# The third state of a gated graph network turned by DMA instead of TensorE, with layer 1 one step later

## The chip, the cores and the metric

The kernel runs on one core of a Trainium2 chip. The metric is the device time of one launch in microseconds (us); for the kernel before, three runs gave a median of 2498.61 us (2496.37 to 2498.63). All times below are in us unless they are marked ns.

## The reference

There are 64 graphs of 256 nodes with 256 features each, and an int32 adjacency per graph. Two pre-norm layers follow one another:

```
h = relu(layernorm(x))
for i in range(3):                       # layer 0: gated graph network, 3 steps
    m    = h @ weight[i]
    aggr = A^T @ m                       # A = (adj != 0)
    h    = gru_cell(aggr, h)             # r, z = sigmoid(..), n = tanh(..); (1-z) n + z h
x = x + h
h = relu(layernorm(x))                   # layer 1: graph attention, 4 heads of 64
v = h W^T + b
l = leaky_relu(v.a_src + v.a_dst, 0.2);  l = -9e15 where adj != 1
x = x + softmax(l) v
```

## The kernel before

**Tiling.** Two graphs form a pair (`PB = 2`), so there are 32 pairs (`NPAIR`) of 512 nodes. The state `hT_a` lies turned, features on partitions and nodes along the free axis (`[128, 2, 512]`), which is what the gate products need. The input `x`, the sum with `aggr` and layer 1 need it by nodes, 128 nodes on the partitions (`[128, 4, 256]`).

**Order.** The order on every engine is written out by hand. `at(tick, phase, p, fn)` files a piece of work under a tick and one of three phases (STEP, READY, REST); at the end all ticks are emitted in order, within a phase the newest pair first. Every engine runs its own instructions in the order in which they are emitted. A step of the gated network takes six ticks (`SUB = 6`, functions `tick_0` to `tick_5`), then `update` writes the new state in place (lines L557 to L559). A pair starts every 18 ticks (`APART`), at `t0 = 18 p`. Its three steps start at t0, t0+12 and t0+24, so the steps of neighbouring pairs fill each other's gaps, and a period of 18 ticks holds three slots. This document calls them:

- slot A, ticks 0 to 5 of the period: the first step of the newest pair
- slot B, ticks 6 to 11: the third step of the pair before it
- slot C, ticks 12 to 17: the second step of the newest pair

Layer 1 of older pairs, and the layer norm and loads of younger ones, are filed into the same ticks.

**Within a step.** TensorE writes gate sums into PSUM banks, and VectorE fills some banks in between: `pe` (L510: `pd + m5`, after which `tick_4` writes into `pd` again) and `pn0`, `pn1` (`first_n`, L526: `(R + 1) * hn`, on top of which `input_n` accumulates). In `tick_5` TensorE's order is `pn0`, `pd`, `pn1`. VectorE also evicts the turned state into `hNlo` (L799) after ScalarE has written `hNhi` (L798). GpSimd makes `hT - n` for the first graph (L541).

**The state by nodes.** After every step `back(l, i)` turns the state by nodes with TensorE, four 128x128 transposes into a bank for each graph (L808, `turn_back`). After the third step `residual` (L814) adds that bank to `x` on VectorE, at ticks t0+31 and t0+32, in slot C.

**Turning by DMA.** For most pairs the normalized input is turned by `plan_turn` in three pieces: `halve` (L387) splits the float32 words into 16-bit halves on VectorE and writes them to DRAM (L389, on SyncE's queue, SP), `turn` reads them back with a DMA transpose (L393), `join` (L399) puts the halves together on VectorE. This is done for layer 0 (`a`) and layer 1 (`b`), with one buffer each for `words` and `turned`.

**Layer 1.** `plan_norm` (L341, L342 statistics; L353 result), `plan_turn`, `values` (L864), `score_rows` (rows to DRAM and back onto all partitions, L893 and L907), `barred_in` and `leaky` (ScalarE), `maxima` (L949, VectorE, two SBUF inputs), `exps` (ScalarE), `output`: `product` on TensorE (L573) and `divided` (L582, L584 on VectorE, L589 on GpSimd). `bar` (L838) makes the mask of absent edges out of a second load of the adjacency; `to_edge` (L764) makes the one for layer 0. `later` moves the ticks of layer 1.

Of the kernel before, what the change touches and what calls it, by code (L numbers as in the profile page):

```python
# [12 lines left out]
U16 = mybir.dt.uint16  # L13
# [5 lines left out]
P = 128  # L19
# [8 lines left out]
def gated_gnn_then_gat_kernel(  # L28
# [39 lines left out]
    nc = tc.nc  # L68
    B, N, D = x.shape
    L = weight.shape[0]  # L70
# [3 lines left out]
    KD = D // P  # L74
    KN = N // P
    PB = 2
    R = PB * KN
    T = PB * N
# [3 lines left out]
    NPAIR = B // PB  # L82
# [6 lines left out]
    dram = ctx.enter_context(tc.tile_pool(name="rows", bufs=2, space=bass.MemoryType.DRAM))  # L89
# [8 lines left out]
    def bank(name):  # L98
        return ps_m.tile([P, 512], F32, tag="mm", name=name)

    BUFS = {
        "x": 5, "adj": 2, "edge": 2, "noedge": 2, "hT_a": 2, "xn": 2, "val": 2, "row": 2, "zz": 4, "o": 2,
    }
# [219 lines left out]
    SUB = 6  # L323
# [3 lines left out]
    def at(tick, phase, p, fn):  # L327
        plan.setdefault(tick, ([], [], []))[phase].append((-p, fn))

    def plan_norm(src, name, p, ticks, relu=False):  # L330


        v = {}

        def stats(r0):
            def fn():
                if not v:
                    v["st"] = small.tile([P, R, 6], F32, tag="st", name=f"st_{name}")
                    v["mv"] = small.tile([P, R, 2], F32, tag="mv", name=f"mv_{name}")
                for r in (r0, r0 + 1):  # L340
                    nc.vector.bn_stats(v["st"][:, r, :], src()[:, r, :])  # L341
                    nc.vector.bn_aggr(v["mv"][:, r, :], v["st"][:, r, :])  # L342
            return fn

        def deviation():
            rstd = v["rstd"] = small.tile([P, R], F32, tag="rstd", name=f"rstd_{name}")
            nc.vector.tensor_scalar_add(rstd, v["mv"][:, :, 1], EPS)
            nc.gpsimd.tensor_tensor(rstd, rstd, mhalf, ALU.pow)

        def result():  # L350
            xn = v["xn"] = buf("xn", [P, R, D], f"xn_{name}")
            for r in range(R):
                nc.vector.tensor_scalar(  # L353
                    xn[:, r, :], src()[:, r, :], v["mv"][:, r, 0:1], 0.0 if relu else v["rstd"][:, r : r + 1],
                    op0=ALU.subtract, op1=ALU.max if relu else ALU.mult,
                )

        for t, fn in zip(ticks, (stats(0), stats(2), deviation, result)):
            at(t, READY, p, fn)
        return v  # L360

    def plan_relu_T(v, tag, name, p, ticks):
# [12 lines left out]

        for k, t in enumerate(ticks):
            at(t, REST, p, fn(k))
        return w

    def plan_turn(src, tag, name, p, ticks):  # L380


        w = {}

        def halve():
            words = buf("words", [P, R, 2, D], f"words_{name}", U16)
            nc.vector.tensor_copy(words, src().bitcast(U16).rearrange("q r (d w) -> q r w d", w=2))  # L387
            w["rows"] = dram.tile([R, P, 2 * D], U16, tag="words", name=f"words_dram_{name}")
            nc.sync.dma_start(w["rows"].rearrange("r q e -> q r e"), words.rearrange("q r w d -> q r (w d)"))  # L389

        def turn():
            w["turned"] = buf("turned", [P, 2, KD * T], f"turned_{name}", U16)
            nc.sync.dma_start_transpose(  # L393
                w["turned"].rearrange("q w (k n) -> q (w k) n", k=KD), w["rows"].rearrange("r q e -> (r q) e")
            )

        def join():
            w["hT"] = buf(tag, [P, KD, T], f"hT_{name}")
            nc.vector.tensor_copy(  # L399
                flat(w["hT"]).bitcast(U16).rearrange("q (n w) -> q n w", w=2), w["turned"].rearrange("q w n -> q n w")  # L400
            )
# [339 lines left out]
    def plan_pair(p):  # L741
        t0 = APART * p
        v = {}
        last = p == NPAIR - 1
        late = p == NPAIR - 2

        def ready(t, fn):
            at(t0 + t, READY, p, fn)

        def step(t, fn):  # L750
            at(t0 + t, STEP, p, fn)

        def rest(t, fn):
            at(t0 + t, REST, p, fn)


        if p == 0:
            v["x"], v["adj"] = first
        else:
            rest(-16, lambda: v.update(x=load_x(p), adj=load_adj(p, "adj")))  # L760

        def to_edge():
            v["edge"] = buf("edge", [P, R, N], f"edge_{p}", F32R)
# [5 lines left out]
        xn_a = plan_norm(lambda: v["x"], f"a{p}", p, [t0 + t for t in norm_ticks])  # L769
        ready(-1 if p else -2.5, to_edge)  # L770
        if dma_a:
            ready(-9.5, lambda: nc.scalar.activation(flat(xn_a["xn"]), flat(xn_a["xn"]), AF.Relu))
            h = plan_turn(lambda: xn_a["xn"], "hT_a", f"a{p}", p, [t0 - 9, t0 - 8, t0 - 3])
        else:
            h = plan_relu_T(xn_a, "hT_a", f"a{p}", p, [t0 - 4, t0 - 3])

# [12 lines left out]
        def back(l, i):  # L789

            def fn():
                if l < L - 1 and i == 0:
                    v["hN"] = node_halves(f"{p}_{l}")
                turn_back(l, i)
                pt = v["pback", i]
                hi, lo = (flat(y[:, i * KN : (i + 1) * KN, :]) for y in v["hN"])
                if l < L - 1:
                    nc.scalar.copy(hi, pt)  # L798
                    nc.vector.tensor_sub(lo, pt, hi)  # L799
                else:  # L800
                    residual(i)
            return fn

        def turn_back(l, i):
            pt = v["pback", i] = bank(f"pback_{p}_{l}_{i}")
            for s in range(KN):
                for k in range(KD):
                    nc.tensor.transpose(  # L808
                        pt[:, s * D + k * P : s * D + (k + 1) * P], h["hT"][:, k, ts(i * KN + s, P)], ident
                    )  # L810

        def residual(i):
            xi = flat(v["x"][:, i * KN : (i + 1) * KN, :])
            nc.vector.tensor_add(xi, v["pback", i], xi)  # L814

        for l in range(L):
            end = last and l == L - 1
            g = Step(f"{p}_{l}", l, lambda: h["hT"], end)
            t = 2 * SUB * l
            ready(t - 3 if l else t - 1, g.state_sums)  # L820
            ready(t + 2, g.last_state_sum)
            step(t, lambda g=g: g.tick_0(v["hN"], v["edge"]))
            for k, fn in enumerate((g.tick_1, g.tick_2, g.tick_3, g.tick_4, g.tick_5), 1):
                step(t + k, fn)
            if not end:
                ready(t + SUB, lambda g=g: g.update(0))
                ready(t + SUB, lambda g=g: g.update(1))
                for i in range(PB):
                    rest(t + SUB + 1 + i, back(l, i))


        def load_adj_1():
# [8 lines left out]
                nc.sync.dma_start(v["noedge_rows"].rearrange("r q t -> q r t"), v["noedge"])  # L841

        rest(16 if last else 22, load_adj_1)
        ready(28 if last else 35, bar)
        if last:
            plan_tail(t0, p, v, g, lambda i: turn_back(L - 1, i), residual)
            return

        dma_b = p < NPAIR - 3
        later = SUB if dma_b else 0  # L850
        xn_b = plan_norm(lambda: v["x"], f"b{p}", p, [t0 + 32, t0 + 33, t0 + 33, t0 + 34], dma_b)
        if dma_b:
# [48 lines left out]
        rows, drow, logits = {}, {}, {}  # L901
# [74 lines left out]
        for y in range(R * H // 2):  # L976
            r, h0 = divmod(2 * y, H)
# [90 lines left out]
```

## Time and profile before

| what | value |
|---|---|
| median of three runs | 2498.61 us |
| profiled execution, its own time | 2498.09 us |
| its span in the profile | 2496.3 us |
| granted TensorE clock | 0.997 |
| TensorE matmul busy | 2464.2 us, 99% |
| TensorE weight load busy | 2191.9 us, 88% |
| VectorE busy | 1992.2 us, 80% |
| ScalarE busy | 1437.5 us, 58% |
| GpSimd busy | 494.3 us, 20% |
| transposes of L808 | 768, of 273 ns each |
| GpSimd sums of L541 (128x512) | 96, of 1479 ns each |
| GpSimd sums of L589 (128x256) | 124, of 1107 ns each |

The duration of a matmul is that of one instruction; matmuls overlap, and so the distance between the starts of neighbours says what each costs. PE stands for TensorE, DVE for VectorE, ACT for ScalarE, POOL for GpSimd, and SPq for SyncE's sequencer. In steady state a period of three slots lasts 75.5 us.

### The profile page before, as it was taken

To read this page: it belongs to the slowest core of one execution; us is meant where nothing else is said; L and a number is where in the kernel's file an instruction comes from. 1 tells how busy PE (TensorE), PEld (TensorE's weight loads), DVE (VectorE), ACT (ScalarE), POOL (GpSimd) and SP (SyncE) were. 2 spreads that over 40 slices of the span, in tenths; PEclk is the share of its full clock that TensorE was granted. 3 is DMA by queue.
4 is the path that set the end of the run, shared out by engine and by line. 5 is a ranking of instruction groups with operands and counts; after the bars stand their busy time and mean duration, and the time that the engine had idled before them with its cause. 6 is when DMAs were issued, how large, how long until landed. Compare 5 with 4: busy or idle time off the path is not lost.

```text
span 2496.3 us, 37566 instructions
## 1 busy us (share of the span) xinstructions
PE 2464.2 (99%) x13446; PEld 2191.9 (88%) x13446; DVE 1992.2 (80%) x4671; ACT 1437.5 (58%) x3007; POOL 494.3 (20%) x419
## 2 busy tenths in 40 slices
PE   8999999999999999999999999999999999999998
PEld 6888888888988888988888988888888889888887
DVE  5678877888877888777888778888778888778767
ACT  3445556555556555566565566565565555665664
POOL 0011121221221121212121212121212222212212
PEclk9999999999999999999999999999999999999999
DMA  3025656455656456656556565556565556564455
GB/s 95 9 68 119 152 119 153 121 127 134 136 127 155 119 126 143 132 131 147 116 131 148 117 146 138 116 130 147 122 153 127 123 132 140 125 157 118 107 109 110
DMA packets 322090, 313.72 MB, mean 126 GB/s; under 512 B 166560, under 2 KB 282224, under 8 KB 321904
## 3 DMA queue, kind: packets, MB, share of 16 engines
q0 software_dynamic: 33728, 130.03, 27.4%
q1 hardware_dynamic: 286608, 181.29, 27.0%
q8 instruction: 106, 1.74, 0.3%
q14 instruction: 80, 0.66, 0.1%
q10 hardware_dynamic: 1568, 0.01, 0.0%
HBM read 215.62 MB, written 56.60 MB: 109 GB/s over the span
## 4 chain that ended last, share of the span: by engine, by line
PE 83%; DVE 12%; ACT 3%; issue 1%; DMA 1%; POOL 0%; SPq 0%; ACTq 0%; DVEq 0%; POOLq 0%
PE pd L313 18%; PE pn L313 13%; PE pc L313 9%; PE po L573 8%; PE pe L313 7%; PE pa L470 5%; PE qb L448 5%; PE p L313 5%; PE pv L864 5%; PE qa L448 4%; PE pback L808 2%; DVE hT_a L559 2%; DVE any L949 2%; DVE R L558 2%; DVE hNlo L799 1%
## 5 line engine op out<-in xcount | busy, mean ns | idle before, releaser
L313 PE MATMUL pn<-aggr,w_a 128*128 128x256 f32 x1536 | 364.9, 380 | 2.8 <-DVE pn L526 2.8
L313 PE MATMUL pd<-T,w_a 128*128 128x256 f32 x1536 | 366.4, 382 | 0.0
L541 POOL TENSOR_TENSOR R<-hT_a,hn 128x512 f32<-128x512 f32 x96 | 141.9, 1479 | 1124.5 <-ACT hn L537 1042.5
L313 PEld LDWEIGHTS pn<-aggr,w_a 128*128 128x128 f32 x1536 | 286.9, 190 | 44.3 <-DVE pn L526 2.1
L313 PEld LDWEIGHTS pd<-T,w_a 128*128 128x128 f32 x1536 | 288.1, 191 | 37.6
L573 PEld LDWEIGHTS po<-val,zz 128*128 128x128 f32 x2048 | 244.9, 192 | 4.5
L537 ACT ACTIVATE hn<-pn,bi 128x256 f32<-128x256 f32 x384 | 160.4, 470 | 145.6 <-PE pn L313 145.4
L589 POOL TENSOR_TENSOR x<-x,o 128x256 f32<-128x256 f32 x124 | 137.1, 1107 | 538.3 <-DVE o L584 538.3
L558 DVE SCALAR_TENSOR_TENSOR R<-Z,R 128x512 f32<-128x512 f32 x192 | 132.5, 690 | 137.9 <-POOL R L541 126.3
L573 PE MATMUL po<-val,zz 128*128 128x65 f32 x2048 | 242.1, 272 | 0.0
L969 ACT ACTIVATE zz<-zz,val 128x256 f32<-128x256 f32 x496 | 223.7, 505 | 0.0
L949 DVE CUSTOM_DVE_ANT_0 any<-drow,noedge 128x256 f32<-128x256 f32 x496 | 209.1, 422 | 9.3 <-DMA drow<-score_dram 0.5
L455 ACT ACTIVATE R<-pc,brz 128x256 f32<-128x256 f32 x192 | 80.5, 470 | 230.8 <-PE pc L313 230.8
L526 DVE SCALAR_TENSOR_TENSOR pn<-R,hn 128x512 f32<-128x512 f32 x192 | 149.1, 777 | 77.3 <-ACT R L455 54.7
L455 ACT ACTIVATE R<-pe,brz 128x256 f32<-128x256 f32 x192 | 80.4, 470 | 213.5 <-PE pe L313 213.5
L313 PE MATMUL pd<-T,w_h 128*128 128x256 f32 x768 | 184.4, 383 | 3.1 <-DVE pe L510 0.4
L313 PE MATMUL pc<-aggr,w_a 128*128 128x256 f32 x768 | 182.5, 381 | 0.0
L313 PE MATMUL p<-T,w_a 128*128 128x256 f32 x768 | 181.9, 379 | 0.6 <-DVE w_a L247 0.6
L313 PE MATMUL pe<-aggr,w_a 128*128 128x256 f32 x768 | 181.4, 379 | 0.0
L313 PE MATMUL pc<-hT_a,w_h 128*128 128x256 f32 x768 | 181.4, 379 | 0.0
L799 DVE TENSOR_TENSOR hNlo<-pback,hNhi 128x512 fp32r<-128x512 f32 x128 | 88.2, 689 | 110.9 <-ACT hNhi L798 110.9
L313 PEld LDWEIGHTS pd<-T,w_h 128*128 128x128 f32 x768 | 143.5, 190 | 32.8 <-DVE pe L510 14.5
(183 smaller groups left out, 5323.0 us busy)
## 6 DMA issues: line engine op xcount, KB each, us to landing
zz<-score_dram POOLq DMA_DIRECT2D x62, 1024.0 KB, 11.0
zz<-topT_dram POOLq DMA_DIRECT2D x62, 1024.0 KB, 7.9
adj<-in_adj_dram SPq DMA_DIRECT2D x64, 512.0 KB
drow<-score_dram SPq DMA_DIRECT2D x62, 512.0 KB
x<-in_x_dram SPq DMA_DIRECT2D x32, 512.0 KB
out_dram<-x SPq DMA_DIRECT2D x31, 512.0 KB
words_dram_a<-words_a SPq DMA_DIRECT2D x30, 512.0 KB
words_dram_b<-words_b SPq DMA_DIRECT2D x29, 512.0 KB
```

The source lines that it names most:

```text
L313: nc.tensor.matmul(pt[:, ts(c, N)], w[:, k, j * D + c * P : j * D + (c + 1) * P], src[:, k, :], start=start and c == 0 and k == 0, stop=(c ...
L448: nc.tensor.matmul(pt, w_n[:, j, :], src, start=start, stop=True, skip_group_check=True)
L455: nc.scalar.activation(of(dst, i)[:, c, :], src[:, c, :], AF.Tanh, bias=brz[:, g0 + c : g0 + c + 1], scale=0.5)
L470: nc.tensor.matmul(pt[:, ts(i, N)], hN[half][:, i * KN + s, ts(e, P)], edge[:, i * KN + s, :], start=(s == 0 and half == 0), stop=(s == KN ...
L526: nc.vector.scalar_tensor_tensor(by_c(self.bank(f"pn{i}")), of(self.R, i), 1.0, of(self.hn, i), op0=ALU.add, op1=ALU.mult)
L537: nc.scalar.activation(n__[:, c, :], p_n[:, c, :], AF.Tanh, bias=bi[:, 2 * KD + c : 2 * KD + c + 1])
L541: nc.gpsimd.tensor_sub(of(self.R, i), of(self.hT(), i), n__)
L558: nc.vector.scalar_tensor_tensor(d_, of(self.Z, i), 1.0, d_, op0=ALU.add, op1=ALU.mult)
L573: nc.tensor.matmul(po[:, ts(h_, VC)], zz[:, j, h_, ts(s, P)], v["val"][:, i * KN + j, ts(h_, VC)], start=(j == 0), stop=(j == KN - 1),)
L589: add(v["x"][:, r, :], v["x"][:, r, :], o)
L949: nc.vector.tensor_tensor_reduce(any_, drow[r // KN][:, h, :], v["noedge"][:, r, :], 1.0, -3.0e38, ALU.add, ALU.max, accum_out=v["top"][:, ...
L969: nc.scalar.activation(zz[:, h, :], zz[:, h, :], AF.Prelu, alpha=ALPHA, bias=v["val"][:, r, S0 + H + h : S0 + H + h + 1],)
```

## The change

For the first 27 pairs (`home`, p < 27) the third state is no longer turned by TensorE. VectorE splits it into halves, the halves go to DRAM, a DMA transpose brings them back by nodes, and VectorE joins them in a buffer of the tag `xn`. GpSimd, instead of VectorE, adds the result to `x`, in one instruction of 128x1024. Layer 1 of these pairs starts six ticks later than before, so each of its pieces moves on by one slot. `bar` comes seven ticks earlier, the pieces of `plan_turn` for layer 0 one tick later. The adjacency has one buffer instead of two, its first load is filed at t0-5 instead of t0-16, and `x` has six buffers instead of five.

```diff
-        "x": 5, "adj": 2, ...
+        "x": 6, "adj": 1, ...
...
-            rest(-16, lambda: v.update(x=load_x(p), adj=load_adj(p, "adj")))
+            rest(-16, lambda: v.update(x=load_x(p)))
+            rest(-5, lambda: v.update(adj=load_adj(p, "adj")))
...
-            h = plan_turn(lambda: xn_a["xn"], "hT_a", f"a{p}", p, [t0 - 9, t0 - 8, t0 - 3])
+            h = plan_turn(
+                lambda: xn_a["xn"], lambda: buf("hT_a", [P, KD, T], f"hT_a{p}"), f"a{p}", p, [t0 - 8, t0 - 7, t0 - 2]
+            )
...
+        home = p < NPAIR - 5
+        if home:
+            h_3 = plan_turn(
+                lambda: h["hT"], lambda: buf("xn", [P, R, D], f"h_{p}"), f"h{p}", p, [t0 + 33, t0 + 34, t0 + 37]
+            )
+            ready(37, lambda: nc.gpsimd.tensor_add(v["x"], v["x"], h_3["hT"]))
...
                 for i in range(PB):
-                    rest(t + SUB + 1 + i, back(l, i))
+                    if not (home and l == L - 1):
+                        rest(t + SUB + 1 + i, back(l, i))
...
-        ready(28 if last else 35, bar)
+        ready(28, bar)
...
-        later = SUB if dma_b else 0
-        xn_b = plan_norm(lambda: v["x"], f"b{p}", p, [t0 + 32, t0 + 33, t0 + 33, t0 + 34], dma_b)
+        later = 2 * SUB if home else SUB if dma_b else 0
+        t_n = t0 + SUB if home else t0
+        ticks = [t_n + (32.5 if home else 32), t_n + 33, t_n + 33, t_n + 34]
+        xn_b = plan_norm(lambda: v["x"], f"b{p}", p, ticks, dma_b)
         if dma_b:
-            hb = plan_turn(lambda: xn_b["xn"], "hT_b", f"b{p}", p, [t0 + 34.1, t0 + 35, t0 + 41])
+            hb = plan_turn(
+                lambda: xn_b["xn"], lambda: buf("hT_b", [P, KD, T], f"hT_b{p}"), f"b{p}", p,
+                [t_n + 34.1, t_n + 35, t_n + 41],
+            )
...
-        rest(37 if dma_b else 36, linked)
+        rest((36, 37, 43)[later // SUB], linked)
```

`plan_turn` itself takes its shapes from its source now (two blocks of 512 for the state, four of 256 for the normalized input); the instructions for `a` and `b` keep their shapes.

More of the change, by code (lines that the diff above doesn't have):

```diff
@@ L101, in gated_gnn_then_gat_kernel @@
     BUFS = {
-        "x": 5, "adj": 2, "edge": 2, "noedge": 2, "hT_a": 2, "xn": 2, "val": 2, "row": 2, "zz": 4, "o": 2,
+        "x": 6, "adj": 1, "edge": 2, "noedge": 2, "hT_a": 2, "xn": 2, "val": 2, "row": 2, "zz": 4, "o": 2,
     }
@@ L378, in plan_relu_T, with plan_turn @@
         return w
-    def plan_turn(src, tag, name, p, ticks):
+    def plan_turn(src, dst, name, p, ticks):
         w = {}
         def halve():
[L386 to L389, printed above, removed]
+            y = src()
+            nb, n = y.shape[1:]
+            words = buf("words", [P, nb, 2, n], f"words_{name}", U16)
+            nc.vector.tensor_copy(words, y.bitcast(U16).rearrange("q b (n w) -> q b w n", w=2))
+            w["rows"] = dram.tile([nb, P, 2 * n], U16, tag="words", name=f"words_dram_{name}")
+            nc.sync.dma_start(w["rows"].rearrange("b q e -> q b e"), words.rearrange("q b w n -> q b (w n)"))
         def turn():
[L392 to L395, printed above, removed]
+            nb, _, n2 = w["rows"].shape
+            w["turned"] = buf("turned", [P, n2 // P, nb * P], f"turned_{name}", U16)
+            nc.sync.dma_start_transpose(w["turned"], w["rows"].rearrange("b q e -> (b q) e"))
         def join():
-            w["hT"] = buf(tag, [P, KD, T], f"hT_{name}")
+            w["hT"] = dst()
             nc.vector.tensor_copy(
-                flat(w["hT"]).bitcast(U16).rearrange("q (n w) -> q n w", w=2), w["turned"].rearrange("q w n -> q n w")
+                flat(w["hT"]).bitcast(U16).rearrange("q (n w) -> q n w", w=2),
+                flat(w["turned"]).rearrange("q (w n) -> q n w", w=2),
             )
```

## The prediction

> **What bounds the kernel now.** I read the engine shares first, then the busy time of the three slots of one period, then VectorE's order of time, then the waits. The first lines are from the page, the others from the table of stretches, whose columns after the length are busy times of PE, PEld, DVE, ACT and POOL, the granted clock, the DMA share and GB/s; the stretches are slots A, B and C of one period.
>
> ```profile
> PE 2464.2 (99%) x13446; PEld 2191.9 (88%) x13446; DVE 1992.2 (80%) x4671; ACT 1437.5 (58%) x3007; POOL 494.3 (20%) x419
> PE 83%; DVE 12%; ACT 3%; issue 1%; DMA 1%; POOL 0%; SPq 0%; ACTq 0%; DVEq 0%; POOLq 0%
> ```
>
> ```profile
> 1206.30:1228.20 21.90, 21.79 (x113) 19.05 (x113) 19.32 (x52) 13.08 (x31) 2.95 (x2) 1.00 0.57 145
> 1228.20:1253.30 25.10, 25.10 (x128) 22.10 (x128) 16.56 (x33) 15.99 (x33) 5.00 (x6) 1.00 0.71 152
> 1253.30:1281.80 28.50, 28.50 (x175) 26.15 (x174) 25.75 (x61) 15.47 (x29) 7.91 (x7) 1.00 0.52 109
> ```
>
> TensorE has no gap worth the name, so whatever leaves it is worth its whole time, as long as nobody makes it wait. But VectorE is at 88% in slot A and 90% in slot C: it is the engine that can make it wait. Where it comes latest shows in the order of time of slot C, which began on TensorE at 1253.31:
>
> ```profile
> 1276.82 1.23 DVE L526 SCALAR_TENSOR_TENSOR pn<-R,hn 128x512 f32<-128x512 f32 x1
> ...
> 1278.37 1.89 PE L313 MATMUL pn<-aggr,w_a 128*128 128x256 f32 x8
> ```
>
> `pn1` is ready at 24.7 us after the slot's start, TensorE wants it at 25.1: 0.3 us of slack. The other place is in slot A, where TensorE waits for `pe` already, once in a period:
>
> ```profile
> PEld pd L313 <- DVE pe L510: 14.5, 29, 0.8
> ```
>
> **What the skill says.** The Trainium skill, "Perfetto Trace Analysis", "Identifying the Most-Contended Engine", judges TensorE by weight-load occupancy, not by matmul time. Here that is 88%, and back-to-back starts agree that it is full. "SBUF — State Buffer", "Who interferes with whom", says that a VectorE instruction with two SBUF inputs contends with a GpSimd instruction that reads SBUF, and that the loser blocks for the whole instruction. The trace before agrees: L526 takes 0.69 alone and 1.23 above, ending 0.56 after GpSimd's L589 ended at 1277.49. A maximum (L949), 0.42 otherwise, took this long beside a GpSimd sum:
>
> ```profile
> 2445.59 1.59 POOL L541 TENSOR_TENSOR R<-hT_a,hn 128x512 f32<-128x512 f32 x1 [9.49 <-ACT hn L537]
> 2445.97 1.49 DVE L949 CUSTOM_DVE_ANT_0 any<-drow,noedge 128x256 f32<-128x256 f32 x1
> ```
>
> It ended 0.28 after the sum. This is the point on which my forecast rests.
>
> **The change part by part.** Durations on VectorE are distances between starts in the order of time of 1200 to 1290 (a 0.69 row occupies 0.61, a 1.22 copy 1.13, two maxima 0.94, one `divided` 0.54, two statistics 1.1).
>
> *TensorE.* 27 pairs lose two groups of four transposes. The chain of waits gives such a group 0.44 us (1258.91, next piece 1259.35): 0.87 us per pair, 23.5 us in all, all of it on the path. The instruction lists of the two kernels confirm 54 groups fewer. The rest of TensorE's work moves: the four `product` groups (1.73 each) from slot C to A, the two `values` groups (1.81 each) from B to C. Undisturbed lengths become A 21.9 + 6.9 = 28.8, B 25.1 - 3.6 = 21.5, C 28.5 - 6.9 + 3.6 - 0.9 = 24.3.
>
> *VectorE.* Per pair it loses two residual sums (0.69 each) and gains `halve` and `join` (1.22 each): +1.07 us. More matters where things stand. Slot A now has `join` of the state, most maxima, the statistics of layer 1 and of the next pair, `xn_b`, `halve` b and all `divided`. Its order, from the instruction list, priced with the rows above: update 3.4, `qb` and T sums to 5.3 (5.2 in slot C before), `join` to 6.4, first maximum to 6.9.
>
> *GpSimd.* Here the new 128x1024 sum starts. The trace has 0.72 for 128x256 (L589 undisturbed) and 1.26 for 128x512 (L541), so 0.54 per 256 columns: 2.34 us. The skill's "GPSIMD Engine Reference", "3.1 Elementwise — side-by-side cycle accounting", has 4497 ns for 2048 columns, half of it 2.25. I take 2.34, to 9.2 us. The second maximum has two SBUF inputs and waits for it, to 9.7. Bounds of that wait: 0, if VectorE is quicker at the lock, and 2.4.
>
> *Slot A, continued.* `hNlo` to 10.3, T4 and `hn` (L502) to 11.4. ScalarE needs that `hn`, then has its own 0.45, one exponential (1.06) and `hNhi` (0.55): 13.4. VectorE has T4n and two maxima meanwhile, then stands until the second `hNlo`, done at 14.0. Without the lock ScalarE would have released the first `hNlo` at 8.2 only, so 1.6 of the 2.3 us is real delay. From 14.0 there is no pause: `divided` 0.54, statistics 1.1, `pe` 0.6 (16.3; wanted at 16.4), T sums 1.28, statistics 1.27, maxima 0.94, `divided` 0.54, `pn0` 0.6 (20.9; wanted at 21.5), Z 0.6, statistics 1.1, `xn_b` 1.05, maxima 0.94, `divided` 0.54, `halve` 1.13: 26.3. `pn1` follows with 0.69, or 1.23 if the GpSimd sum of `divided` stands beside it as before: 27.0 to 27.5. TensorE wants it at 25.1. **Wait in slot A: 1.9 to 2.4, taken 2.15.**
>
> *Slot B.* It has TensorE's order of slot A before, where VectorE was 0.27 late with `pe`. Between `hn` and T4n now stands `xn_a` (1.29), while 0.54 of waiting for ScalarE disappears and the update begins some 0.25 earlier, because no mask stands ahead of it: 0.5 later. **Extra wait: 0.5** (0.3 to 0.7).
>
> *Slot C.* VectorE loses `halve` b, `xn_b`, statistics, maxima and `divided`, and gains two `values` evictions, `halve` of the state and `score`. It stood idle 3.1 us at the end of the same TensorE order in B; the masks and T sums filed there (3.0) fit. Taken as 0.
>
> *Loads and buffers, at nothing.* The adjacency load (filed at tick 13) has four ticks, over 15 us, before `to_edge` at tick 17; 512 KB at the 210 GB/s and more that stretches of 1 us show takes 2.5. With one buffer it stands behind `bar` at tick 10, which is done. Should that cover go, `edge` is late, and TensorE's first sums of slot A wait. The mask's two buffers are kept from tick 28 to the maxima of tick 62, before the next user at 64; the sixth `x` covers the six ticks that `x` lives longer. ScalarE's pieces move a slot; GpSimd's row additions (L930) stand behind the new sum, issued near 9.3 and 10.6, landing 11 later, 6 us before slot B reads them.
>
> *SP's queue.* Two more issues a pair: the write (0.39) and the transpose (1.4 to 5.3 of issuing). The transpose of the state stands behind the score rows and behind `join` a, which frees `turned`: about 19.8 us into C. `join` asks for it 5.3 into A, 9.6 us later. In the trace DMA activity after a transpose issue at 1282.11, with two more transfers behind it, ended before 1288.4: at most 6.3. The skill's "DMA: Bandwidth & Descriptors", "Latency and other measured facts", has 261 GB/s for a transpose, an estimate of 2.0 us for 512 KB. So no wait, with 3 us to spare; `words` is free for the same reason.
>
> *Sum.* -0.87 + 2.15 + 0.5 = +1.78 us per pair, times 27: +48 on the profiled execution's 2498.1 (span 2496.3 and 1.8 around it): 2546. The median of the runs is 0.5 above that execution, nothing beside this.
>
> **The rivals.**
> - *TensorE's saving stays.* The sum on GpSimd gets its lock where VectorE has single-input work, and `pn1` is in time: 2474.6 at best, to 2490 with 0.3 us of waits a pair. For it: TensorE is 83% of the chain, and the layer 1 work moves as a block. Against: VectorE's count for slot A has no room. It decides at `pn1` ending by 25.1 us.
> - *No lock, but the queue.* The maximum isn't held up: `pn1` ends at 25.4 to 25.9, a wait of about 0.6, with slot B's 0.5 and -0.87: +0.23 per pair, 2504 (2493 to 2516).
> - *The transpose lands late.* If 256 rows of 1024 halves take over 9.6 us from issue, VectorE stands at `join`, and each us beyond costs 27: 2573 at 1, 2627 at 3. For it: the issue alone took up to 5.3. Against: the 6.3 above.
> - *Not what it says* is excluded: the transposes are gone from the list.
>
> **How the numbers follow.** Lock as worked out 0.60 (its own range, waits of 1.4 to 2.6 in A: 2520 to 2564); saving stays 0.14; queue alone 0.16 (split 0.03 faster, 0.06 same, 0.07 slower); transpose late 0.10. A measurement can tell about 0.2%, 5 us. So faster 0.17, same 0.06, slower 0.77. The range 2490 to 2580 leaves out most of the saving case and the transpose over 1.3 us late.
>
> **What would show it.** Right: a new POOL row of 128x1024 near 2.3 us; a maximum right after `join` of 2 us or more in place of 0.42; waits of PE for DVE `pn`, 2 us long, 27 times in place of 2, and for `pe` larger than 14.5; L808 at 552 transposes. Slots A, B, C near 31, 22, 24.3. Wrong: a period under 75.5 us, or VectorE idle ahead of `join` with the DMA named as releaser.

## The result and the profile after

| | before | after |
|---|---|---|
| median of the runs (six each) | 2498.3 us | 2583.15 us (2560.25 to 2591.26) |
| ratio | | 1.032 [1.0271, 1.0369] |
| profiled execution, its own time | 2498.09 us | 2562.16 us |
| its span | 2496.3 us | 2560.4 us |
| slots A, B, C in steady state | 21.89, 25.07, 28.52 | 30.29, 22.20, 24.46 |
| period | 75.48 us | 76.95 us |

The change is slower by 3.2%, 85 us; the profiled execution alone is 64.1 us longer. The forecast was 2546 us with a range of 2490 to 2580: the profiled execution lies inside it, the median 3 us above its upper end. Slot lengths, here and below, are distances between the first `qa` matmuls of neighbouring slots.

The engine shares and the chain of the page after:

```profile
PE 2461.2 (96%) x13230; PEld 2170.9 (85%) x13230; DVE 2044.2 (80%) x4671; ACT 1441.3 (56%) x3007; POOL 572.4 (22%) x446
...
PE 53%; DVE 36%; ACT 6%; DMA 3%; issue 2%; SPq 0%; POOL 0%; DVEq 0%; POOLq 0%; ACTq 0%
```

TensorE has 216 instructions fewer, and its share fell from 99% to 96%: it waits now. In the chain TensorE fell from 83% to 53%, and VectorE rose from 12% to 36%. The table of stretches for one period, slots A, B and C (columns as before: PE, PEld, DVE, ACT, POOL, granted clock, DMA share, GB/s):

```profile
1220.84:1251.13 30.29, 28.78 (x176) 26.09 (x174) 27.08 (x70) 15.59 (x30) 12.19 (x9) 1.00 0.64 148
1251.13:1273.32 22.19, 21.78 (x113) 19.02 (x113) 19.92 (x46) 14.03 (x32) 2.38 (x2) 1.00 0.35 92
1273.32:1297.78 24.46, 24.44 (x121) 21.22 (x120) 16.50 (x30) 15.02 (x31) 4.22 (x3) 1.00 0.79 186
```

Slot A now carries both the most TensorE work and the most VectorE work, 27.1 of 30.3 us, and it is where TensorE lacks 1.5 us. The order of time of that slot shows the reason. First what happens after `join` of the state (VectorE and GpSimd):

```profile
1226.07 1.22 DVE L401 COPY h<-turned_h 128x2048 uint16<-128x2048 uint16 x1
...
1227.20 0.42 DVE L969 CUSTOM_DVE_ANT_0 any<-drow,noedge 128x256 f32<-128x256 f32 x1
1227.37 2.48 POOL L828 TENSOR_TENSOR x<-x,h 128x1024 f32<-128x1024 f32 x1 [6.59 <-DVE h L401]
...
1227.66 2.46 DVE L969 CUSTOM_DVE_ANT_0 any<-drow,noedge 128x256 f32<-128x256 f32 x1
```

The second maximum takes 2.46 in place of 0.42 and ends 0.27 after the GpSimd sum, which took 2.48. The end of the slot, VectorE with one line of GpSimd, and then TensorE:

```profile
1245.16 1.22 DVE L390 COPY words_b<-xn_b 128x2048 uint16<-128x2048 uint16 x1
...
1245.32 1.64 POOL L592 TENSOR_TENSOR x<-x,o 128x256 f32<-128x256 f32 x1 [3.63 <-DVE o L587]
...
1246.29 1.22 DVE L529 SCALAR_TENSOR_TENSOR pn<-R,hn 128x512 f32<-128x512 f32 x1
```

```profile
1247.57 1.99 PE L313 MATMUL pn<-aggr,w_a 128*128 128x256 f32 x8 [1.51 <-DVE pn L529]
1264.47 1.99 PE L313 MATMUL pd<-T,w_h 128*128 128x256 f32 x8 [0.41 <-DVE pe L513]
```

`pn1` comes 26.7 us after the start of the slot, right behind `halve`; TensorE wanted it at 25.2 and waits 1.51. Here the two engines meet a second time: `pn1` has two SBUF inputs, starts while GpSimd's sum of `divided` (L592) is running and takes 1.22. `pn0` of the same slot starts ahead of its sum (1240.42 against 1240.58) and takes 0.69; there the sum takes longer, 1.10 in place of 0.72. The second line of the last fence is the wait for `pe` in slot B. The view of waits, summed over the launch (us, times, longest):

```profile
PEld pn L313 <- DVE pn L529: 67.5, 31, 11.1
PEld pd L313 <- DVE pe L513: 24.3, 29, 1.9
```

**Where the 64.1 us went.** Marks of the slots give it by stretches: 3.5 up to slot B of the fourth period; 37.6 in the 25 periods of steady state (1.5 each); 22.6 in the six slots that follow, where the last `home` pair gives way to the five that have the old layout; 0.4 behind them. These six slots take 151.0 before and 173.6 after. The last two of the three shown here hold most of the loss, 68.5 against 50.4:

```profile
2255.30:2280.50 25.20, 25.20 (x130) 22.14 (x130) 20.67 (x51) 16.85 (x35) 2.01 (x2) 1.00 0.24 76
2280.50:2315.90 35.40, 23.87 (x111) 20.07 (x110) 20.08 (x49) 13.22 (x29) 7.50 (x7) 0.86 1.11 155
2315.90:2349.00 33.10, 30.49 (x176) 27.62 (x175) 22.38 (x60) 19.32 (x41) 6.02 (x5) 0.95 0.32 81
```

In the first of the two, a slot C, the DMA share is 1.11, against 0.24 in the slot B ahead of it. The order of time shows what is in it, on GpSimd's queue and on SP's:

```profile
2280.81 1.23 POOL L950 DMA_DIRECT2D zz<-score_dram  x1
2282.81 1.20 POOL L950 DMA_DIRECT2D zz<-score_dram  x1 [0.77 <-ACT zz L942]
2283.66 1.59 POOL L950 DMA_DIRECT2D zz<-topT_dram  x1
2296.47 1.23 POOL L950 DMA_DIRECT2D zz<-topT_dram  x1
```

```profile
2282.07 6.73 SPq L397 DMA_TRANSPOSE turned_a<-words_dram_a  x1
2288.85 0.70 SPq L115 DMA_DIRECT2D adj<-in_adj_dram  x1
```

Each of the four additions moves 1024 KB. Pair 26 is the last with `later` = 12 and pair 27 the first with 6, so the second additions of the one (ticks 536 and 537 of the launch) and the first of the other (535 and 536, which a `later` of 12 would put at 541 and 542) meet in one slot; behind them stand the transpose for pair 30's first layer and its adjacency. Who pays is in the next lines (VectorE, then TensorE), and in the chain of waits over this stretch:

```profile
2307.51 1.23 DVE L401 COPY hT_a<-turned_a 128x2048 uint16<-128x2048 uint16 x1 [9.08 <-DMA turned_a<-words_dram_a]
2318.51 0.69 DVE L768 TENSOR_SCALAR edge<-adj 128x1024 fp32r<-128x1024 int32 x1 [6.17 <-DMA adj<-in_adj_dram]
```

```profile
2312.40 3.78 PE L313 MATMUL pn<-aggr,w_a 128*128 128x256 f32 x8 [10.73 <-DVE pn L529]
```

```profile
2288.85 29.64 DMA adj<-in_adj_dram
```

`join` a waits 9.08, and as VectorE works in order, `pn` stands behind it: TensorE waits 10.73. Then it waits again for `edge`, because the adjacency took 29.64 from issue to landing. Not all of the 22.6 is waiting, though: layer 1 that had moved one slot later meets layer 1 that had not, and even in the cleanest passage of the runs below (e11) the six slots take 156.2, 5.2 more than before.

### The profile page after: what moved, and what is told of

It reads as the page before. It is cut to its first block, busy times and chain, and to the rows that moved or that the text cites. A ratio compares the mean times of both kernels' runs of the same rounds, so it can differ in the third digit from the quotient of the medians.

```text
span 2560.4 us, 37216 instructions
## 1 busy us (share of the span) xinstructions
PE 2461.2 (96%) x13230; PEld 2170.9 (85%) x13230; DVE 2044.2 (80%) x4671; ACT 1441.3 (56%) x3007; POOL 572.4 (22%) x446
## 4 chain that ended last, share of the span: by engine, by line
PE 53%; DVE 36%; ACT 6%; DMA 3%; issue 2%; SPq 0%; POOL 0%; DVEq 0%; POOLq 0%; ACTq 0%
PE pd L313 12%; PE pn L313 11%; DVE any L969 6%; PE pc L313 6%; PE pv L884 4%; PE pe L313 4%; PE pa L473 3%; PE po L576 3%; PE p L313 3%; PE qb L451 3%; DVE hNlo L805 3%; PE qa L451 2%; DVE pn L529 2%; DVE hT_a L562 2%; DVE R L561 1%
## 5 line engine op out<-in xcount | busy, mean ns | idle before, releaser
L313 PE MATMUL pn<-aggr,w_a 128*128 128x256 f32 x1536 | 374.4, 387 | 56.5 <-DVE pn L529 55.9
L544 POOL TENSOR_TENSOR R<-hT_a,hn 128x512 f32<-128x512 f32 x96 | 148.9, 1551 | 1090.2 <-ACT hn L540 622.4
L313 PEld LDWEIGHTS pd<-T,w_a 128*128 128x128 f32 x1536 | 288.2, 191 | 37.6
L969 DVE CUSTOM_DVE_ANT_0 any<-drow,noedge 128x256 f32<-128x256 f32 x496 | 263.2, 531 | 8.8
L592 POOL TENSOR_TENSOR x<-x,o 128x256 f32<-128x256 f32 x124 | 135.8, 1096 | 348.2 <-DVE o L587 343.9
L313 PEld LDWEIGHTS pd<-T,w_h 128*128 128x128 f32 x768 | 143.5, 190 | 42.6 <-DVE pe L513 24.3
L454 ACT ACTIVATE hn<-qb,bhn 128x256 f32<-128x256 f32 x192 | 90.7, 473 | 142.9 <-DVE hn L505 131.7
L313 PEld LDWEIGHTS pc<-aggr,w_a 128*128 128x128 f32 x768 | 146.6, 191 | 20.2
## 6 DMA issues: line engine op xcount, KB each, us to landing
zz<-score_dram POOLq DMA_DIRECT2D x62, 1024.0 KB, 12.2
```

The source lines that it names most:

```text
L313: nc.tensor.matmul(pt[:, ts(c, N)], w[:, k, j * D + c * P : j * D + (c + 1) * P], src[:, k, :], start=start and c == 0 and k == 0, stop=(c ...
L454: nc.scalar.activation(of(self.hn, i)[:, c, :], pt, AF.Identity, bias=bhn[:, c : c + 1])
L544: nc.gpsimd.tensor_sub(of(self.R, i), of(self.hT(), i), n__)
L592: add(v["x"][:, r, :], v["x"][:, r, :], o)
L969: nc.vector.tensor_tensor_reduce(any_, drow[r // KN][:, h, :], v["noedge"][:, r, :], 1.0, -3.0e38, ALU.add, ALU.max, accum_out=v["top"][:, ...
```

## The experiments

The theory: the lost time per pair has three terms, the lock of the GpSimd sum, the new order of VectorE's work, and TensorE's saving against them; the rest is the changeover. The rivals were late transposes of the state and the GpSimd queue. Steady slot lengths of all runs, the two changeover slots of the profile above (C and A), and medians:

| kernel | A | B | C | period | changeover C, A | median, us | ratio to before |
|---|---|---|---|---|---|---|---|
| before | 21.89 | 25.07 | 28.52 | 75.48 | 28.52, 21.88 | 2498 | |
| after | 30.29 | 22.20 | 24.46 | 76.95 | 35.44, 33.03 | 2583.2 | 1.032 [1.0271, 1.0369] |
| e1_sum_vector | 29.5 to 35.1 | 22.19 | 24.46 | varies | 40.74, 34.51 | 2586.6 | 1.0361 [1.0319, 1.0403] |
| e2_no_sum | 29.21 | 22.19 | 24.46 | 75.86 | 41.87, 34.28 | 2558.3 | 1.0243 [1.0201, 1.0286] |
| e3_sum_quarters | 29.26 | 22.19 | 24.46 | 75.91 | 25.62, 29.74 | 2537.5 | 1.0179 [1.0149, 1.021] |
| e4_late_only | 29.21 | 22.19 | 25.28 | 76.68 | 33.61, 34.23 | 2556.6 | 1.0239 [1.0218, 1.026] |
| e10_maxima | 29.24 | 22.19 | 24.46 | 75.89 | 32.99, 29.06 | 2532.4 | 1.0149 [1.0096, 1.0202] |
| e7_order | 28.52 | 21.94 | 24.46 | 74.92 | 44.31, 29.02 | 2516.9 | 1.0073 [1.0049, 1.0096] |
| e9_early | 30.30 | 22.20 | 24.46 | 76.96 | 40.71, 28.55 | 2566.7 | 1.0267 [1.0241, 1.0294] |
| e8_spread | 30.30 | 22.20 | 24.46 | 76.96 | 27.09, 28.77 | 2566.2 | 1.0267 [1.0242, 1.0292] |
| e5_pair30_tensor | 30.29 | 22.20 | 24.46 | 76.95 | 24.59, 28.55 | 2560.2 | 1.0243 [1.0226, 1.0259] |
| e11_all | 28.52 | 22.23 | 24.46 | 75.21 | 24.49, 28.56 | 2498.8 | 1.000 [0.9988, 1.0012] |
| e12_order_early_pair30 | 28.52 | 21.93 | 24.46 | 74.91 | 24.59, 28.55 | 2493.7 | 0.9978 [0.9967, 0.9989] |
| e13_order_pair30 | 28.52 | 21.93 | 24.46 | 74.91 | 24.59, 28.55 | 2494.0 | 0.9982 [0.9967, 0.9997] |

For e2 the floor of slot A is given; it reached up to 32.4. In the new layout the cleanest passage of the two changeover slots is 24.5 and 28.6; the slots beside them can lose as well, which is said below. The slot lengths are from one execution of each kernel. In the steady slots that is enough, as they repeat 25 times; the changeover comes once, and the kernels that don't aim at it (after, e1, e2, e3, e4, e7, e9, e10) took from 55.4 us (e3) to 76.2 (e2) for its two slots. A single value of these columns is thus one draw, and 22.6 us is not a fixed price.

**e1, the sum on VectorE.**

```diff
-            ready(37, lambda: nc.gpsimd.tensor_add(v["x"], v["x"], h_3["hT"]))
+            ready(37, lambda: nc.vector.tensor_add(v["x"], v["x"], h_3["hT"]))
```

> The changed kernel, with the sum of the state and x on VectorE instead of GpSimd, at the same place. In the changed kernel slots A, B, C take 30.29, 22.20 and 24.46 us, a period of 76.94 (75.48 before). Lock theory: the GpSimd sum holds the second maximum up for 2 us; a VectorE sum costs 1.13 in its place, so slot A falls to 29.2 to 29.6, the period to 75.8 to 76.2, some 20 to 30 us off the whole. Queue theory (slot A of VectorE is simply too long): the sum adds 1.1 to that queue, slot A rises to 31 or more, the period to 77.8 or more. Both: the loss of some 20 us at the change to the last five pairs stays.

The median is 2586.6, not better than after. The sum takes 1.22 and the maxima behind it 0.42 each: the lock is gone. But its slot A is irregular, because another wait came in (VectorE's view of waits):

```profile
DVE h L401 <- DMA turned_h<-words_dram_h: 38.7, 25, 3.3
```

The transpose of the state landed late in 25 periods, by up to 3.3 us, so the forecast for the lock alone can't be read from this run. In the profile after the same wait is 0.5 us in all. The edit itself is the likely reason. In after, GpSimd issues the first score addition of 1024 KB behind its sum, 8.9 us or more into slot A and so behind `join`; without the sum on GpSimd nothing holds it back, and it leaves 0.1 ahead of slot A (1156.48 in this period), while the transpose is under way:

```profile
1156.36 1.19 POOL L950 DMA_DIRECT2D zz<-score_dram  x1
```

e2 is the only other kernel that turns the state by DMA and has no sum on GpSimd: there too the addition leaves 0.1 ahead of the slot and the transpose is late 25 times. In the ten traces with both the sum on GpSimd and the state turned by DMA the addition leaves 8.8 or later, and `join` waits at most four times, never over 0.81. No run delayed the additions alone, so this cause is an agreement of twelve traces and not an experiment.

**e2, no sum, and e3, the sum in four instructions.** e2 leaves the addition of the third state to `x` out. In e3 it is four GpSimd instructions of 128x256.

```diff
-            ready(37, lambda: nc.gpsimd.tensor_add(v["x"], v["x"], h_3["hT"]))
+            for r in range(R):
+                ready(37, lambda r=r: nc.gpsimd.tensor_add(v["x"][:, r, :], v["x"][:, r, :], h_3["hT"][:, r, :]))
```

> The changed kernel without the sum of the state and x (left out, so x goes on without the state). Lock theory: no maximum takes over 0.5 us any more, slot A falls to 28.4 to 28.9, the period to 75.0 to 75.6, level with before or a little under. Queue theory: pn1 is late without the sum too, slot A stays over 29.8 and the period over 76.5. Both: the loss at the change to the last five pairs stays, so the total stays over the kernel before by 10 us or more.

> The changed kernel with the GpSimd sum in four pieces of 128x256 (0.72 us each where undisturbed) instead of one of 128x1024. Lock theory: the lock is given back between the pieces, so a maximum waits for 0.7 at most; the longest maximum falls from 2.48 to 1.2 or less, slot A to 29.0 to 29.9, the period to 75.6 to 76.5. If it is GpSimd's whole working time that counts, or the queue: no gain, period 76.9 or more, since four pieces take 2.9 in place of 2.4.

Slot A falls to 29.21 without the sum, and to 29.26 with the same sum in quarters. The order of time of e3 (VectorE, GpSimd):

```profile
1212.02 3.54 POOL L829 TENSOR_TENSOR x<-x,h 128x256 f32<-128x256 f32 x4 [6.59 <-DVE h L401]
...
1212.31 0.83 DVE L970 CUSTOM_DVE_ANT_0 any<-drow,noedge 128x256 f32<-128x256 f32 x1
```

GpSimd is busy for longer, 3.54 in place of 2.48, and yet the maximum takes 0.83 in place of 2.46: VectorE gets in after one quarter. So what costs time is how long one instruction of the other engine is, not how much it does. The lock is worth 30.29 - 29.21 = 1.08 us a period. e2's slot A was expected at 28.4 to 28.9, so a part of the loss stayed; e7 below says what it can be. e2's execution had late transposes as in e1, 32.5 us of waits, and so its median doesn't price the lock.

**e10, the maxima a tick later.** The maxima are filed behind `hNlo` and `hn`, so that none of them stands beside the sum.

```diff
-            ready(43 + later + y if not late else 45 + (3 * y) // 8, maxima(r, h0))
+            ready(43 + later + home + y if not late else 45 + (3 * y) // 8, maxima(r, h0))
```

(`shift` and `shift_rows` likewise.)

> The changed kernel with the maxima of the changed pairs, and what follows from them, one tick later, so that none stands right behind join when GpSimd's sum begins; the sum stays one instruction of 128x1024. Lock theory: the longest wait of a maximum goes, slot A falls to 29.0 to 29.5, as without the sum (29.21), the period to 75.7 to 76.2. Rival: T4 (L504), with two SBUF inputs as well, waits in its place, slot A stays at 30 or more.

Slot A is 29.24, with the GpSimd sum whole and at its place (2.37). That is the lock undone by order alone, and it gives 1.05 us, about what leaving the sum out gives. It also shows why a maximum that is held up by 2.04 costs only that much. In e10 VectorE stands idle during the sum until ScalarE releases `hNlo` (slot A began at 1131.34):

```profile
1139.47 0.69 DVE L805 TENSOR_TENSOR hNlo<-pback,hNhi 128x512 fp32r<-128x512 f32 x1 [1.69 <-ACT hNhi L804]
```

That is 8.13 into the slot; in after, behind the held maximum, `hNlo` starts at 9.22, which is 1.09 later. The rest of the 2.04 would have been a wait for ScalarE anyway.

**e4, layer 1 later, the state turned by TensorE as before.** `h_3` and its sum are taken out, and `back(2, i)` is restored for all pairs; the rest is as in after.

> The changed kernel with the third state turned by TensorE and added by VectorE in slot C as before; layer 1 stays two steps late, buffers and mask stay as changed. Lock theory: slot A loses the join and the lock, pn1 is in time: 28.4 to 28.9; slot C 25.3; slot B keeps its wait for pe (22.2); period 75.9 to 76.4, 0.4 to 0.9 over before. Queue theory (the moved layer 1 alone fills slot A): slot A over 29.5, period over 77. The loss of some 20 us at the change to the last five pairs belongs to the move of layer 1, so it stays: total 2525 to 2545.

The period is 76.68, and A is longer than the 28.4 to 28.9 expected: moving layer 1 by a slot, with the new ticks and buffers that go with it, costs 1.20 us a period with none of the DMA path of the state there. Against after, C is 25.28 instead of 24.46, so the transposes that TensorE loses are worth 0.82; and A is 29.21, as with the lock gone. The three terms add up: 1.20 for the moved work, -0.82 for TensorE, +1.08 for the lock, 1.46 in all; measured 76.95 - 75.48 = 1.47.

**e7, another order of VectorE.** Three pieces are filed a tick later: `xn_b` and `halve` b behind `pn1` in slot A, and `xn_a`, the norm of the next pair's first layer (with ScalarE's relu behind it), behind `pe` in slot B.

```diff
-        norm_ticks = (-14, -13, -13, -10) if dma_a else ...
+        norm_ticks = (-14, -13, -13, -9) if dma_a else ...
...
-            ready(-9.5, lambda: nc.scalar.activation(...
+            ready(-8.5, lambda: nc.scalar.activation(...
...
-        ticks = [t_n + (32.5 if home else 32), t_n + 33, t_n + 33, t_n + 34]
+        ticks = [t_n + (32.5 if home else 32), t_n + 33, t_n + 33, t_n + (35 if home else 34)]
...
-                [t_n + 34.1, t_n + 35, t_n + 41],
+                [t_n + (35 if home else 34.1), t_n + 35, t_n + 41],
```

> The changed kernel with three pieces of VectorE's order moved behind what TensorE waits for: xn_b and halve b behind pn1 in slot A (2.2 us), xn_a behind pe in slot B (1.3 us). Nothing is added or taken away. Queue theory (TensorE waits because of what stands ahead of pn1 and pe, 1.5 and 0.4 us): slot A falls from 30.29 to 28.8 to 29.1, slot B from 22.20 to 21.7 to 22.0, the period to 74.9 to 75.5, even with the lock still there. Rival: VectorE is simply full there, the moved 2.2 us make the update and pe of slot B late: slot B 23 or more, period 76 or more.

The period is 74.92, less than before. In slot A of e7 (VectorE):

```profile
1198.02 2.46 DVE L969 CUSTOM_DVE_ANT_0 any<-drow,noedge 128x256 f32<-128x256 f32 x1
...
1214.45 0.69 DVE L529 SCALAR_TENSOR_TENSOR pn<-R,hn 128x512 f32<-128x512 f32 x1
...
1216.90 1.13 DVE L353 TENSOR_SCALAR xn_b<-x,mv_b 128x256 f32<-128x256 f32 x4
1218.07 1.23 DVE L390 COPY words_b<-xn_b 128x2048 uint16<-128x2048 uint16 x1
```

The lock on the maximum is still there, 2.46, and costs nothing: `pn1` no longer stands behind 2.4 us of work that nobody waits for, and comes 24.0 into the slot. With `halve` no longer between, it also starts ahead of GpSimd's sum (1214.45 against 1214.62) and takes 0.69 in place of 1.22: the second meeting falls out the other way. In e4 and e10, where the first meeting is gone, `pn1` still takes 1.22 to 1.23 and TensorE still waits 0.42 to 0.45 for it, less than the 0.53 of the meeting. So the 0.7 us between their slot A and e7's is the queue, this second meeting, or both; no run takes them apart. The median is still above before, for the changeover takes 44.31 in slot C; SP's line there is the longest issue of a transpose in the study:

```profile
2229.48 21.63 SPq L397 DMA_TRANSPOSE turned_a<-words_dram_a  x1
```

**e8, e9, e5: the changeover and the transposes.** e8 files pair 27's score additions and `leaky` three ticks later. e9 files the pieces of `plan_turn` a tick earlier, for layer 0 and for the state. e5 turns pair 30's layer 0 input by TensorE.

```diff
+        apart = 3 if p == NPAIR - 5 else 0
...
-        rest(43 + later, add_rows(0, "score"))
-        rest(44 + later, add_rows(1, "score"))
+        rest(43 + later + apart, add_rows(0, "score"))
+        rest(44 + later + apart, add_rows(1, "score"))
```

```diff
-                ... f"a{p}", p, [t0 - 8, t0 - 7, t0 - 2]
+                ... f"a{p}", p, [t0 - 8, t0 - 7, t0 - 3]
...
-                ... f"h{p}", p, [t0 + 33, t0 + 34, t0 + 37]
+                ... f"h{p}", p, [t0 + 32, t0 + 33, t0 + 37]
```

```diff
-        dma_a = p >= 2
+        dma_a = p >= 2 and p != NPAIR - 2
```

> The changed kernel with the score additions and the leaky pieces of pair 27, the first that isn't changed, three ticks later, away from the additions of pair 26 and the transposed load of pair 30. Pile-up theory: at the change to the last five pairs two pairs' additions to zz (four of them) and a transpose share the DMA engines in one slot C, and join a and the adjacency come late; apart, that slot C falls from 35.4 to 27 or less, the slot A after it from 33.0 to 31 or less, 8 to 12 us off the total; the steady slots stay 30.29, 22.20, 24.46. Rival (VectorE's queue, two pairs' layer 1 in one slot): the two slots stay within 2 us of what they are.

> The changed kernel with the transpose of the state some 5 us earlier: join a at t0-3 instead of t0-2, which frees the buffer, halve of the state a tick earlier, so that the transpose is issued ahead of the score rows. Late-transpose theory (executions of the changed kernel differ by 30 us because the transpose of the state lands up to 3 us after join asks for it, in some executions 25 times): join never waits for that DMA, slot A stays at 30.3 in all periods, the runs lie within 12 us of each other, at 2555 to 2570. Rival (the spread comes from the change to the last five pairs alone): the spread stays 25 us or more.

> The changed kernel with the normalized input of pair 30 alone turned by TensorE instead of through DRAM. In the changed kernel its transpose, in the slot C in which the additions of pairs 26 and 27 meet, made join wait 9.1 us, and the two slots there took 35.4 and 33.0 us. Pile-up theory: without that transpose the first falls to 22.5 to 26, the second to 29 to 33 (the adjacency load may still be late), 10 us or more off the loss of some 20; steady slots unchanged, the total still 2545 to 2585 because of the late transposes of the state. Rival (something else of that slot is late as well, the row loads or VectorE): the slot stays over 30.

e8 takes the crowd, four additions of two pairs in one slot, apart: the transpose issues in 1.90 at the place where the seven kernels with the crowd (after, e1, e2, e3, e4, e7, e9) took 6.4 to 21.6, `join` of pair 30 doesn't wait, where six of those seven waited 7.3 to 18.0, and slots C and A are 27.09 and 28.77 in place of 35.44 and 33.03. The lengths alone would not show it: e3 went through the crowd, with an issue of 7.42, in 25.62 and 29.74, as its transpose landed in time. In e10 only the two score additions stand ahead of the transpose, and it still took 10.65. In e8 10.4 us turn up in the next slot C (39.37 in place of 28.96), where ScalarE waits for an addition:

```profile
2371.40 0.91 ACT L990 ACTIVATE zz<-zz,val 128x256 f32<-128x256 f32 x2 [8.84 <-DMA zz<-topT_dram]
```

e5 takes away the transpose that suffers instead: 24.59 and 28.55, and the three other kernels with this edit (e11, e12, e13) have 24.5 to 24.6 and 28.6 as well. In e5 the next slot C grows to 34.97, as `join` of pair 31 waits 5.6 us, and from the start of the last slot to the end it takes 77.1 where after takes 70.3, so that the profiled execution is only 1.4 shorter. Both halves of the reading are borne out, then: TensorE pays through `join`, by four traces, and the crowd of additions delays the transpose, by the one trace of e8 against seven. Neither edit alone brought the loss back, for nearly as much turned up in other slots; why it did so is not shown, and in e11 to e13, which have e5's edit too, the next slot C is 28.96.

e9's forecast was that the transposes of the state are never late and that the runs lie within 12 us of each other, at 2555 to 2570. Both came true (2564.9 to 2570.7). It did not help at the changeover: 40.71 in slot C, with a `join` wait of 13.9.

**e11, all of it** (e7, e9, e10, e5).

> All remedies at once: the orders of slots A and B (as in e7_order), the earlier transpose of the state (as in e9_early), the maxima a tick later (as in e10_maxima), pair 30 turned by TensorE. If the parts add up: slots A, B, C near 28.5, 21.9 and 24.5, a period of 74.9 where before has 75.48, so 14 us gained over 25 periods; the change to the last five pairs loses 3 to 10 in place of 20 to 40; total 2485 to 2498, a little under the kernel before or level with it. If the moved pieces get into each other's way: slot B over 22.5, total over 2505.

It is level with before: 1.000 [0.9988, 1.0012]. The changeover is clean, but the period is 75.21 and not 74.9: slot B grew by 0.3. In it two maxima now stand directly ahead of `pn0`, for which TensorE waits (VectorE, then TensorE; slot B began at 1146.37):

```profile
1162.05 0.42 DVE L969 CUSTOM_DVE_ANT_0 any<-drow,noedge 128x256 f32<-128x256 f32 x1
...
1162.40 0.69 DVE L529 SCALAR_TENSOR_TENSOR pn<-R,hn 128x512 f32<-128x512 f32 x1
```

```profile
1163.24 1.96 PE L313 MATMUL pn<-aggr,w_a 128*128 128x256 f32 x8 [0.35 <-DVE pn L529]
```

In e12, which differs by e10's shift alone, there are three small operations on `top` in that place, and slot B is 21.93. The shift makes the rows of `topT` late as well: GpSimd waits for them 168.0 us in all, against 16.6 in after. That is not what lengthens slot B, for in e10 GpSimd waits 137.1 and slot B is 22.19 as in after.

**e12 and e13, without e10's shift** (e7, e5, and in e12 also e9).

> The order of e7, both transposes a tick earlier as in e9, pair 30 turned by TensorE as in e5, and no shift of the maxima. If the parts add: the period of e7, 74.9 (A 28.5, B 21.9, C 24.5), so 25 x (75.5 - 74.9) = 14 us less than before in the steady part, and a changeover of 24.5 / 28.6 / 29 to 35 that costs 0 to 6 us against before: total 2484 to 2494, ratio 0.994 to 0.998. If the shift of the maxima was what let the changeover be clean in e11, slot C after pair 30 takes about 35, as in e5, and the total is 2492 to 2498. If two transposes issued a tick earlier disturb the score rows as in e11 (POOL waiting for topT_dram), B is 22.2 and the total 2497 to 2503.

> As e12 without the earlier transposes: a period of 74.9 and the same changeover. If late transposes of the state are what spreads the runs, these runs spread over 10 us or more and the median is 3 to 15 us above e12; if the earlier transposes only cost (score rows filed later), this one is faster than e12 by up to 6 us, total 2482 to 2490.

Both have the period 74.91, and e12 has the lowest median of the study, faster than before by 0.22% (interval 0.11% to 0.33%); e13 by 0.18%, interval barely clear of zero. The runs don't tell e13 from e12, so the earlier transposes bring nothing that these runs can show, and the spread of the runs is about 20 us in both. In e12 the 25 periods bring 13.5 us and the start 2.4, of which the six slots of the changeover take 10.6 back (161.6 against 151.0). The loss sits one slot A earlier than in after, 35.95 long, in a load of `x` (VectorE):

```profile
2193.07 0.43 DVE L341 BATCH_NORM_STATS2 st_a<-x 128x6 f32<-128x256 f32 x1 [8.42 <-DMA x<-in_x_dram]
```

## Why the prediction was right, and where it was not

**The direction and the mechanism hold; the size is in part luck.** The forecast of +48 had only the loss per pair in it. Of the profiled execution's +64.1 that loss is 37.6, less than forecast, and a loss that the forecast did not have makes up the difference and more. The prediction named the lock of the GpSimd sum, `pn1` in slot A and `pe` in slot B. The sum is 2.48 (forecast 2.34), the maximum behind `join` 2.46 (2 or more), TensorE waits for `pn` 31 times and for `pe` 24.3 in place of 14.5; slots are 30.3, 22.2 and 24.5 (31, 22, 24.3). The rule that it took from the Trainium skill, "SBUF — State Buffer", "Who interferes with whom", that one instruction holds the shared ports as a whole, is what e3 shows most plainly: the maximum's 2.46 became 0.83 when the sum came in quarters.

**Term by term, for one period:**
- *TensorE's saving*, forecast 0.87: measured 0.82, e4 against after.
- *The real delay by the lock*, forecast 1.6: measured 1.08, e2 and e10 against after. The wait at `pn1` was forecast at 2.15 and is 1.51. That ScalarE would release the first `hNlo` at 8.2 was right (8.13); the end of the held maximum was not, as `hNlo` behind it starts at 9.22 and not at 9.8. `pn1` came at 26.7 us, not at 27.0 to 27.5: the GpSimd sum starts 0.1 after `join` ends, beside the first maximum, and the second `hNlo` was done 13.5 us into the slot and not 14.0.
- *The queue without the lock*, forecast as a wait of 0.6: A is 29.21 without the lock and 28.52 once the order is changed, 0.7 in all. But it is not shown to be the queue alone, since `pn1` meets a GpSimd sum there (1.22 for 0.69; the prediction had 0.69 or 1.23). The undisturbed length was forecast at 28.8.
- *Slot B*, forecast 21.5 + 0.5 = 22.0: measured 22.20; e7's 21.94 shows that about 0.3 of it was to be had by order.
- *Slot C*, forecast 24.3: measured 24.46.
- *Sum*, forecast +1.78: measured +1.47 in steady state.

**The step that failed is the one that multiplied.** The sum took 1.78 for 27 pairs and nothing else. The 25 steady periods gave 37.6 us, where 1.78 each would be 44.5. What the prediction had no term for is the changeover from 27 pairs of one layout to five of the other, 22.6 us in the profiled execution. Its two claims on DMA fail there: "at nothing" for loads and buffers (the adjacency took 29.64 from issue to landing, where 2.5 was reckoned and over 15 was the cover), and "no wait" on SP's queue, where the transpose for pair 30 landed 9 us late. For the transposes of the state "no wait" held in after (0.5 us in all), though they are issued 7.8 to 8.5 us before `join` asks, not 9.6. The text did say who would pay if that cover went: `edge` late, TensorE's first sums of slot A waiting. That is the 6.17 us wait for the adjacency in the profile after, but as a warning and not as a term. The "11 later" reckoned for the landing of a row addition came from the median of the page (11.0 for the score rows before, 12.2 after), which says nothing of four in one slot.

**The median** lies 21 us above the profiled execution, where the prediction expected half a us between the two, and so it left the range. What made four of after's six runs take 2580 to 2591 stays open, since the one that has a trace took 2562. The third rival, a late transpose of the state, was given 27 us for each us of delay. It is absent in that trace, and it came 25 times only in e1 and e2, where the edit lets the additions go early, so nothing shows that it made after's longer runs. The other candidate is the changeover, whose two slots vary by 21 us among the kernels that don't aim at it. The four runs each of e5, e8 and e9 lie within 2.7, 9.7 and 5.8 us, which fits either; e12 and e13 spread over 20 and 23.

**The rival "saving stays"** was priced at 2474.6 to 2490 and said to be decided by `pn1` ending at 25.1. (The 2490 goes with 0.57 of waits a pair; the 0.3 that stands beside it gives 2483.) e7 shows the condition to be the right one: with `pn1` in time the period is 0.56 below before. It was turned down on a count that took VectorE's order as given; three filings were enough to change it. What keeps e12 at 2494 is mostly the changeover: with e11's passage of it, 156.2 in place of 161.6, e12's execution would take 2489 by this sum, inside that rival's range.

## What to carry to other kernels

When work moves between slots, price the order of the engine that feeds the busiest one: in slot A VectorE had the time, but 2.4 us that nobody waited for stood ahead of what TensorE wanted. A long GpSimd instruction beside two-input VectorE work costs by its length, so cut it, or put single-input work there. When an instruction is taken off an engine, look at what stood behind it in the queue: without the sum GpSimd issued its additions 9 us earlier. And where a change applies to some iterations only, look at the seam between the two layouts before multiplying: in the profiled execution it cost as much as 15 periods.

## What the runs showed that was not expected

- The issue of a DMA transpose on SP's queue has no fixed price. Transposes of `turned` took 1.4 to 5.3 us in the trace before. Beside the four additions of 1024 KB one took 6.73 in after, 10.08 in e9 and 21.63 in e7, and 1.90 at the same place in e8 with two of the additions moved away. What stands behind it on the queue waits as long.
- After its long waits TensorE ran at half pace: eight matmuls of `pn` took 3.78 after a wait of 10.73, and 3.75 after 5.42 in e12, against 1.99 after 1.51. The Trainium skill, "TensorE: Matmul & The Clock Gate", "What's actually happening", says that an idle window of about 3.4 us halves the clock. These two waits agree, and each cost about 1.8 us more than its length. Between 2 and 4 us the length of the wait does not decide it: the eight took 1.99 after 3.88 in e10, and 3.50 after 2.65 in e8 where e3 has 1.99 after the same 2.65.
